# Two layers of adapters, attention and routed experts on one core: second expert products in seven quarter products, first adapter matrix in four pieces

## The chip, the cores and the metric

The kernel runs on 1 core of one Trainium2 chip. The metric is the device time in microseconds (us) of one execution. Three runs of the kernel before took 1205.24, 1205.88 and 1206.55 us; the median is 1205.88 us.

A core has a matrix engine (TensorE, PE in the profile; PEld is its loading of weights), VectorE (DVE), ScalarE (ACT), GpSimd (POOL) and SyncE (SP, which only starts transfers here). Each engine works through its own instructions in order. They wait for each other by counters: an instruction that needs another engine's result waits until that engine's counter has reached a number. TensorE writes its results into an accumulation memory (PSUM), from which VectorE or ScalarE fetch them.

## The reference

`x` is 8 sequences of 128 rows by 512, in f32, as everything here. Cut to what matters:

```python
# layer 0: one adapter matrix of eight per sequence, then a base matrix with 8 experts (2 per row)
c = einsum('bsi,boi->bso', x, weight[adapter_ids])
x = x + (c @ base_w.T + base_b + 2 * experts(c))
# layer 1: attention with 32 heads over a paged cache of 512 and the row itself, then 64 small experts
y = attention(x, ...)                                      # 8 x 128 x 512
scores = (y @ Wq_w.T) @ keys.T                             # 64 experts
gate = softmax over the 16 best, 0 elsewhere
z = (y @ A_w.T) * gate, each expert's gate over its 8 columns   # first product, 8 x 128 x 512
x = x + 2 * (z @ B_w.T)                                    # second product and residual
```

The last line is the second product of the title: eight products of 128x512 by 512x512, to which the rows that layer 0 left are added.

## The kernel before, in words

**Layer 0** (the head, the first 120 us or so). Eight sequences `b` are worked off in eight steps `t`. `l0_load(b)` starts the transfers of the transposed rows `xT` and of the adapter matrix `wt` (1 MB, its number read from `ids` into a register); for `b == 0` the matrix comes in three pieces (256, 256 and 512 KB), all by SP's queue, and `xT` by ACT's. On PE stand per step the adapter products (L626, `cp`), the transposed expert row of the step before (L683, `ltp`), its product (L689) and the base products (L643, L648). On VectorE stand the gate of the two experts (L653 to L671, ending with `low`, which L683 turns), then the sum `x1` (L691) and its scale. Between them lie pieces of side work: `l0_rows` (L567 to L571) computes the row numbers for the value cache from `vpg`, and `l0_angles(0..3)` computes the angles for the rotation from `leni` and `fr`. `l0_small` has POOL start the transfers of `leni`, `fr`, `vpg` and `nw` in this order, behind the sum of rows and bias (L677). At t = 1 the order on VectorE is gate, `l0_rows`, one product on `nw`, `l0_angles(0)`.

**Layer 1.** 64 units `u` (a sequence and a head group each) run as a pipeline written out by hand: `iteration(u)` holds scores, softmax, exchange through DRAM, values and output products of up to four units. PE is fed without a break by this order. The last iterations (`u` = 64 to 66, NU is 64) hold the rest of the pipeline and the experts of layer 1 for seven of eight sequences: `f_turn` (transposed rows, L857), `f_project` (first product, L866), `f_gate` (the gate on VectorE, L877 to L899). The gated `z` of sequences 0 to 5 is transposed by an exchange through DRAM (`z_blocks`, `z_exchange`), and `z_turn` copies it on ScalarE (L393) to the form that PE takes; that of 6 and 7 is transposed on PE (L919). `spare` is the memory of the layer's transposed input `xo`, free by then.

**The tail** (from 1171.7 us). `f_second(t)` is the second product of one sequence: 4 matmuls of 128 columns by 512 into one PSUM tile, then on VectorE `ot = op + x1` (L1452), with the rows `x1` loaded by SP shortly before (L1421), and a store by SP (L1455). The tiles come from the tags "o" and "y" in turn. The last sequence goes in two halves of 256 columns, each into a tile of its own and with its own sum and store. Between the products stand `f_turn`, `f_project` and `f_gate` of sequence 7, and the transposes of 6 and 7. An f32 matmul stands in the profile as two records: the 4 matmuls of a sequence are 8.

PSUM is given out in tiles: `bank(tag)` is 128x512 f32 for one of the tags "o", "y", "q", "kv"; `banks()` is twice that, for one of two places in turn. The framework puts the waits between engines into the program, by the tiles that instructions read and write.

## Time and profile before

| | |
|---|---|
| median of 3 runs | 1205.88 us |
| profiled execution: its time, its span | 1209.55 us, 1207.8 us |
| PE busy in the span | 1194.7 us (99%) |
| VectorE, ScalarE, POOL busy | 913.1, 504.3, 740.4 us |
| granted TensorE clock | 1.000 |
| DMA, mean | 250 GB/s |
| PE's idle time, startup included | 13.1 us |

The span is the time from the first to the last instruction of the profiled execution; its time is longer by 1.75 us, and it is one of the slower executions (the median is 3.67 us below it). A row of a timeline has start, duration, engine, line, operation, what is written from what, shape, and behind it in brackets the idle time before and what ended it. Since matmuls are pipelined, the start of one and the start of the next lie closer together than the duration of one: 16 records of 128x128 in 1.95 us, where one takes 0.28.

### The profile page before, as it was taken

The numbers are of one execution on the slowest core, as the hardware profiler recorded it, in microseconds if no ns is written. First come the engines' busy times: TensorE is split into PE (matmuls) and PEld (weight loads), VectorE is DVE, ScalarE is ACT, GpSimd is POOL, SyncE is SP. The second block draws the span as 40 slices with busy tenths as digits, with TensorE's granted clock in tenths as the row PEclk, the third lists the DMA queues.
The fourth block names the chain that finished last, engine by engine and source line by source line (L and its number), as shares of the span: only waits on it lengthen the run. The fifth ranks groups of instructions, "written<-read, shape, count | busy, mean of one in ns | idle before, by whom it ended". The sixth has DMA issues, their size and how long they took to land.

```text
span 1207.8 us, 16783 instructions
## 1 busy us (share of the span) xinstructions
PE 1194.7 (99%) x4156; PEld 714.6 (59%) x4156; DVE 913.1 (76%) x2103; ACT 504.3 (42%) x1457; POOL 740.4 (61%) x828
## 2 busy tenths in 40 slices
PE   9999999999999999999999999999999999999998
PEld 7666545565555556555556555555656555555554
DVE  2647788787888787878887887879887888787632
ACT  1345534443444444444444444444444444443211
POOL 3545769778755686578647685687657784643100
PEclk9999999999999999999999999999999999999999
DMA  8823777888888988888789978887989888898742
GB/s 315 287 89 113 247 238 245 263 265 264 264 253 257 301 244 278 260 287 282 237 258 282 294 240 281 285 289 246 279 255 302 254 263 251 261 281 230 232 140 97
DMA packets 205300, 302.31 MB, mean 250 GB/s; under 512 B 84755, under 2 KB 119316, under 8 KB 204180
## 3 DMA queue, kind: packets, MB, share of 16 engines
q1 hardware_dynamic: 170308, 196.81, 53.2%
q10 hardware_dynamic: 18576, 52.04, 13.6%
q0 software_dynamic: 16320, 52.40, 12.4%
q8 instruction: 33, 0.54, 0.2%
q14 instruction: 63, 0.52, 0.1%
HBM read 185.44 MB, written 115.74 MB: 249 GB/s over the span
## 4 chain that ended last, share of the span: by engine, by line
PE 82%; DMA 6%; POOL 4%; DVE 3%; issue 2%; SPq 1%; ACT 1%; ACTq 0%; DVEq 0%; POOLq 0%
PE o L956 18%; PE p L262 18%; PE s L439 16%; PE y L1081 13%; PE s L442 4%; PE p L295 3%; DMA px<-pb 2%; PE op L1445 2%; PE y L1094 2%; PE bp L648 1%; PE cp L626 1%; DMA kt<-in_kc 1%; PE fr L866 1%; POOL p L469 1%; DVE pb L474 1%
## 5 line engine op out<-in xcount | busy, mean ns | idle before, releaser
L463 ACT ACTIVATE p<-p,low 128x640 f32<-128x640 f32 x256 | 211.8, 828 | 433.7 <-DVE den L468 267.4
L469 POOL TENSOR_SCALAR p<-p,den 128x640 f32<-128x640 f32 x256 | 210.2, 822 | 233.4 <-DVE den L468 232.5
L452 DVE CUSTOM_DVE_ANT_0 p<-s,mask,rs 128x640 f32<-128x640 f32 x256 | 222.3, 878 | 81.6 <-PE s L442 80.7
L262 PE MATMUL p<-wqkv,xo 128*128 128x384 f32 x784 | 281.1, 487 | 0.7 <-DVE c L265 0.3
L439 PE MATMUL s<-kt,qkT 128*128 128x512 f32 x504 | 258.7, 595 | 4.5 <-DMA kt<-in_kc 2.6
L956 PE MATMUL o<-pT,vt 128*128 128x512 f32 x512 | 230.2, 592 | 0.0
L474 DVE STREAM_TRANSPOSE pb<-p 128x640 f32<-128x640 f32 x248 | 204.8, 826 | 25.6 <-POOL p L469 25.5
L1081 PE MATMUL y<-wo,oT 128*128 128x256 f32 x784 | 206.6, 380 | 0.9 <-DVE yp L1168 0.5
L262 PEld LDWEIGHTS p<-wqkv,xo 128*128 128x128 f32 x784 | 148.2, 190 | 70.2 <-POOL wqkv L163 1.6
L442 PEld LDWEIGHTS s<-qkT 128*128 128x128 f32 x504 | 95.8, 190 | 120.5 <-issue 120.5
L203 POOL DMA_INDIRECT vt<-in_vc,vrow x128 | 137.6, 1075 | 40.8 <-issue 31.9
L956 PEld LDWEIGHTS o<-pT,vt 128*128 128x128 f32 x512 | 97.2, 190 | 107.8 <-issue 92.8
L439 PEld LDWEIGHTS s<-kt,qkT 128*128 128x128 f32 x504 | 94.2, 190 | 78.3 <-issue 32.5
L1081 PEld LDWEIGHTS y<-wo,oT 128*128 128x128 f32 x784 | 131.9, 191 | 9.8 <-PE s L442 1.2
L311 ACT ACTIVATE sq<-c 128x128 f32<-128x128 f32 x320 | 98.8, 309 | 9.5 <-DVE oT L474 1.4
L442 PE MATMUL s<-qkT 128*128 128x128 f32 x504 | 96.8, 274 | 0.0
L317 POOL TENSOR_TENSOR rs<-ss,mhalf 128x5 f32<-128x5 f32 x64 | 82.2, 1284 | 5.3
L979 ACT COPY oT<-o 128x512 f32<-128x512 f32 x64 | 37.4, 585 | 102.3 <-PE o L956 77.2
L315 POOL TENSOR_SCALAR ss<-ss,eps 128x5 f32<-128x5 f32 x64 | 27.6, 431 | 74.3 <-ACT sq L311 74.3
L956 PE MATMUL o<-pT,vn 128*128 128x512 f32 x128 | 65.4, 592 | 0.0
L425 DVE STREAM_TRANSPOSE pb<-ca 128x640 f32<-128x640 f32 x60 | 50.2, 836 | 18.1 <-DMA px<-pb 8.2
L265 DVE TENSOR_TENSOR c<-c,p 128x384 f32<-128x384 f32 x84 | 44.9, 534 | 22.9 <-PE p L262 22.7
(198 smaller groups left out, 1441.3 us busy)
## 6 DMA issues: line engine op xcount, KB each, us to landing
pT<-px SPq DMA_DIRECT2D x64, 1280.0 KB, 6.6
px<-pb SPq DMA_DIRECT2D x120, 400.0 KB, 5.2
px<-pb ACTq DMA_DIRECT2D x120, 400.0 KB, 4.2
qkb<-px SPq DMA_DIRECT2D x60, 320.0 KB, 3.4
kt<-in_kc SPq DMA_DIRECT2D x512, 32.0 KB, 5.1
wqkv<-in_wqkv POOLq DMA_DIRECT2D x32, 384.0 KB, 4.8
wo<-in_wo POOLq DMA_DIRECT2D x17, 512.0 KB, 7.5
yd<-yp POOLq DMA_DIRECT2D x12, 512.0 KB, 9.0
```

What stands on the lines that cost most here:

```text
L203: nc.gpsimd.indirect_dma_start(out=kv_t[step][1][:, c, :], out_offset=None, in_=vc, in_offset=bass.IndirectOffsetOnAxis(ap=vrow[:, hf, at ...
L262: nc.tensor.matmul(out=ps, lhsT=xo[:, pr, x, c, :], rhs=w[:, c, :], start=(c == 0), stop=(c == 1))
L311: nc.scalar.activation(sq, cs[:, at : at + D], AF.Square, accum_out=ss[:, h : h + 1])
L317: nc.gpsimd.tensor_tensor(rs, ss, mhalf, ALU.pow)
L439: nc.tensor.matmul(out=s[:, :L], lhsT=qkT[:, h, :], rhs=kt[:, :, g % GH, :], start=True, stop=True)
L442: nc.tensor.matmul(out=s[:, L:NK], lhsT=qkT[:, h, :], rhs=qkT[:, REP, :], start=True, stop=True)
L452: nc.vector.tensor_tensor_reduce(out=p, in0=s_t.pop((u, h))[:, :NK], in1=mask_t[st], scale=rs_t[u][:, h : h + 1], scalar=BIG, op0=ALU.add, ...
L463: nc.scalar.activation(p, p, AF.Exp, bias=low, scale=-1.0, accum_out=den)
L469: nc.gpsimd.tensor_scalar(p_t[u, h], p_t[u, h], den, 1.0, ALU.mult, ALU.mult)
L474: nc.vector.transpose(pb_t[u][:, :, h * w : (h + 1) * w].rearrange("p i (j a) -> p j i a", a=32), p_t.pop((u, h)).rearrange("p (j i a) -> ...
L956: nc.tensor.matmul(out=o, lhsT=vt[:, c, j * D : (j + 1) * D] if c < LC else vn_t.pop(u), rhs=pT[:, c], start=(c == 0), stop=(c == LC),)
L1081: nc.tensor.matmul(out=y_t["y"][:, half * HN : (half + 1) * HN], lhsT=part(key)[:, i * S : (i + 1) * S], rhs=wo_t[:, slot(w, key[0] // (B ...
```

## The change

In the **head**, the first adapter matrix comes in four pieces of 256 KB, the first and third by SP's queue and the second and fourth by ACT's, each engine with the matrix number in a register of its own. And `l0_rows` moves from t = 1 to t = 2, behind `l0_angles`.

In the **tail**, the second products are computed for pairs of sequences. The `z` of a pair stands as four quarters (two sequences by two halves of the inner 512), the matrix as four quarters (two halves of the inner by two of the outer 512); seven products of sums of quarters, M1 to M7, give what eight quarter products gave (Strassen's scheme in Winograd's form). `f_quarters` computes four sums of the matrix on POOL at u = 64, `z_sums(p)` four sums of the pair's `z` on POOL. `f_product(p, n)` is one product: 2 matmuls by 256 columns into half a PSUM tile, then on VectorE one sum that adds the result to one to four of the pair's residual quarters, in place. The residual rows are loaded into `spare` in iterations 65 and 66. Each pair takes one `banks()` tile for its first four products, a "o" tile for the next two and a "y" tile for the last.

```diff
-            a = nc.sync.value_load(ids[0:1, b : b + 1])
-            at = (0, P, 2 * P, DM) if b == 0 else (0, DM)
-            for n, end in zip(at, at[1:]):
-                nc.sync.dma_start(
+            both = (nc.sync, nc.scalar) if b == 0 else (nc.sync,)
+            which = [e.value_load(ids[0:1, b : b + 1]) for e in both]
+            at = range(0, DM + 1, P if b == 0 else DM)
+            for i, (n, end) in enumerate(zip(at, at[1:])):
+                both[i % len(both)].dma_start(
...
-            if t == 1:
+            if 1 <= t <= 4:
+                l0_angles(t - 1)
+            if t == 2:
                 l0_rows()
                 nc.vector.tensor_scalar_mul(nw[:, 0, :], nw[:, 0, :], -SCALE)
-            if 1 <= t <= 4:
-                l0_angles(t - 1)
...
+    def f_quarters():
+        b = fw_t["b"]
+        q11, q12, q21, q22 = (b[:, 2 * i : 2 * i + 2, j * HN : (j + 1) * HN] for i in (0, 1) for j in (0, 1))
...
+        tt = nc.gpsimd.tensor_tensor
+        tt(t3, q22, q12, ALU.subtract)
+        tt(t2, t3, q11, ALU.add)
+        tt(t4, q21, t2, ALU.subtract)
+        tt(t1, q12, q11, ALU.subtract)
+        fw_t["q"] = [q11, q21, q22, t4, t1, t2, t3]
+
+    def z_sums(p):
...
+        a11, a12, a21, a22 = a[:, :2], a[:, 2:], b[:, :2], b[:, 2:]
+        tt = nc.gpsimd.tensor_tensor
+        tt(s1, a21, a22, ALU.add)
+        tt(s2, s1, a11, ALU.subtract)
+        tt(s4, a12, s2, ALU.subtract)
+        tt(s3, a11, a21, ALU.subtract)
+        zs_t[p] = [a11, a12, s4, a22, s1, s2, s3]
...
+                for b in range(4 * z, 4 * z + 4):
+                    f_load_x(b)
...
+            if u == NU:
+                f_quarters()
...
-                nc.vector.tensor_tensor(
-                    ot[:, k : k + n], op[:, k : k + n], x1[:, k : k + n], ALU.add
+        INTO = {
+            M1: slice(0, 4),
+            M2: slice(0, 1),
+            M3: slice(1, 2),
+            M4: slice(2, 3),
+            M5: slice(1, 4, 2),
+            M6: slice(1, 4),
+            M7: slice(2, 4),
+        }
+
+        def f_product(p, n):
+            halves = at_t.setdefault(p, [])
+            if not halves:
+                two = banks(f"op_{p}")
+                halves += [two[:, i * HN : (i + 1) * HN] for i in range(4)]
+                for tag in ("o", "y"):
+                    t = bank(tag, f"op_{p}{tag}")
+                    halves += [t[:, :HN], t[:, HN:]]
+                halves.pop()
+            ps = halves.pop(0)
+            for c in range(2):
+                nc.tensor.matmul(
+                    out=ps,
+                    lhsT=zs_t[p][n][:, c, :],
+                    rhs=fw_t["q"][n][:, c, :],
...
+            x1 = spare[:, (TURNED + 2 * p) * DM : (TURNED + 2 * p + 2) * DM]
+            o = x1.rearrange("p (k n) -> p k n", k=4)[:, INTO[n]]
+            nc.vector.tensor_tensor(o, o, ps.unsqueeze(1).to_broadcast([P, o.shape[1], HN]), ALU.add)
...
+        def begin(p):
+            for n in (M1, M2, M4, M5):
+                f_product(p, n)
+
+        def end(p):
+            for n in (M6, M3, M7):
+                f_product(p, n)
+            f_store(2 * p)
+            f_store(2 * p + 1)
...
+        z_sums(1)
+        begin(0)
+        yT = f_turn(b7, sb, psum)
+        end(0)
+        z_sums(2)
+        ps = f_project(b7, yT, sb, psum)
+        f_gate(b7, *ps, sb, psum)
+        begin(1)
+        end(1)
+        for b, tag in ((b7 - 1, "q"), (b7, "kv")):
+            z_turn(b, p2.tile([P, NC, S], F32, tag=f"zT{b}", name=f"fzT_{b}"), tag)
+        begin(2)
+        end(2)
+        z_sums(3)
+        for n in (M1, M2, M6, M5, M7, M3):
+            f_product(3, n)
+        f_store(6)
+        f_store(7, 1)
+        f_product(3, M4)
+        f_store(7, 0)
```

More of the change, by code (lines that the diff above doesn't have):

```diff
@@ L504, in l0_load @@
             wt = wt_home.pop(b)
-            a = nc.sync.value_load(ids[0:1, b : b + 1])
-            at = (0, P, 2 * P, DM) if b == 0 else (0, DM)
-            for n, end in zip(at, at[1:]):
-                nc.sync.dma_start(
+            both = (nc.sync, nc.scalar) if b == 0 else (nc.sync,)
[3 more added lines that the diff above has]
+                both[i % len(both)].dma_start(
                     out=wt.rearrange("p o n -> p (o n)")[:, NC * n : NC * end],
-                    in_=w0[ds(a, 1), :, NC * n : NC * end].rearrange("e p n -> p (e n)"),
+                    in_=w0[ds(which[i % len(both)], 1), :, NC * n : NC * end].rearrange("e p n -> p (e n)"),
                 )
@@ L905, in f_gate, with z_turn, f_load_x @@
         zg_t[b] = zg
-    zT_t = {}
+    zT_t, zs_t, x1_t = {}, {}, {}
     TURNED = B - 2
-    def z_turn(b, sb):
+    def z_turn(b, zT, tag=None):
         zg = zg_t.pop(b)
         if b < TURNED:
-            zT = zT_t[b] = sb("zT", [P, NC, S])
             turn_chunks(zT, zg)
-            return
-        tp = bank("q" if b % 2 else "kv", f"ztp_{b}")
-        for c in range(NC):
-            nc.tensor.transpose(tp[:, c * S : (c + 1) * S], zg[:, c * P : (c + 1) * P], ident)
-        zT = sb("zT", [P, NC, S])
-        nc.scalar.copy(zT.rearrange("p c s -> p (c s)"), tp)
-        zT_t[b] = zT
+        else:
+            tp = bank(tag, f"ztp_{b}")
+            for c in range(NC):
+                nc.tensor.transpose(tp[:, c * S : (c + 1) * S], zg[:, c * P : (c + 1) * P], ident)
+            nc.scalar.copy(zT.rearrange("p c s -> p (c s)"), tp)
+        zT_t[b] = zT
+    def f_load_x(b):
+        at = (TURNED + b) * DM
+        x1_t[b] = spare[:, at : at + DM]
+        nc.sync.dma_start(out=x1_t[b], in_=x1_d[ORDER[b]])
+    def f_quarters():
+        b = fw_t["b"]
+        q11, q12, q21, q22 = (b[:, 2 * i : 2 * i + 2, j * HN : (j + 1) * HN] for i in (0, 1) for j in (0, 1))
+        room = [wo_t[:, i].rearrange("p (t c n) -> p t c n", t=2, c=2) for i in (3, 6)]
+        t3, t2, t4, t1 = (room[i // 2][:, i % 2] for i in range(4))
+        tt = nc.gpsimd.tensor_tensor
[5 more added lines that the diff above has]
+    def z_sums(p):
+        a, b = zT_t.pop(2 * p), zT_t.pop(2 * p + 1)
+        at = p % 3 * 2 * DM
+        room = spare[:, at : at + 2 * DM].rearrange("p (k c s) -> p k c s", k=4, c=2)
+        s1, s2, s3, s4 = (room[:, i] for i in range(4))
+        a11, a12, a21, a22 = a[:, :2], a[:, 2:], b[:, :2], b[:, 2:]
[5 more added lines that the diff above has]
+        zs_t[p] = [a11, a12, s4, a22, s1, s2, s3]
+    spare = xo.rearrange("p r x c s -> p (r x c s)")
     with ExitStack() as l1:
@@ L1247, in adaln_ffn_kernel @@
         }
-        spare = xo.rearrange("p r x c s -> p (r x c s)")
         written_t = {}
@@ L1306, in iteration @@
                 z = u - NU - 1
-                z_turn(z, lambda n, shape: wo_t[:, slot(T4, NQ - 1), z * DM : (z + 1) * DM].rearrange("p (c s) -> p c s", c=NC))
+                z_turn(z, wo_t[:, slot(T4, NQ - 1), z * DM : (z + 1) * DM].rearrange("p (c s) -> p c s", c=NC))
+                for b in range(4 * z, 4 * z + 4):
+                    f_load_x(b)
             if u >= NU:
                 z_blocks(u - NU + 4)
+            if u == NU:
+                f_quarters()
             if u in (2, 3):
@@ L1402, in adaln_ffn_kernel @@
         sm = l2.enter_context(tc.tile_pool(name="f_s", bufs=3))
-        x1_t, first_t = {}, {}
-        def home(b):
-            def sb(n, shape):
-                pool = p2 if n in ("yT", "zg", "zT") else sm
-                return pool.tile(shape, F32, tag=n, name=f"f{n}_{b}")
-            t = banks(f"fp_{b}")
-            def psum(n, shape):
-                v = t[:, DM : DM + shape[1]] if n == "z" else t[:, :DM] if n == "tp" else t[:, : shape[1]]
-                return v.rearrange("p (c s) -> p c s", c=NC) if n == "tp" else v
-            return sb, psum
@@ L1419, in f_load_x @@
-        def f_load_x(b):
-            x1 = p2.tile([P, DM], F32, tag="x1", name=f"fx1_{b}", bufs=4)
-            nc.sync.dma_start(out=x1, in_=x1_d[ORDER[b]])
-            x1_t[b] = x1
-        def f_begin(b):
-            sb, psum = home(b)
-            first_t[b] = f_turn(b, sb, psum), sb, psum
-        def f_first(b):
-            yT, sb, psum = first_t.pop(b)
-            f_gate(b, *f_project(b, yT, sb, psum), sb, psum)
-        def f_turn_z(t):
-            b = t
-            sb = lambda n, shape: p2.tile(shape, F32, tag=n, name=f"f{n}_{b}")
-            z_turn(b, sb)
@@ L1437, in f_second @@
-        def f_second(t):
-            b = t
-            zT, x1 = zT_t.pop(b), x1_t.pop(b)
-            ot = p2.tile([P, DM], F32, tag="ot", name=f"ot_{t}")
-            n = DM // 2 if t == B - 1 else DM
-            for k in range(0, DM, n):
-                op = bank("kv" if k else "y" if t % 2 else "o", f"op_{t}_{k}")
-                for c in range(NC):
-                    nc.tensor.matmul(
-                        out=op[:, k : k + n],
-                        lhsT=zT[:, c, :],
-                        rhs=fw_t["b"][:, c, k : k + n],
-                        start=(c == 0),
-                        stop=(c == NC - 1),
-                    )
-                nc.vector.tensor_tensor(
-                    ot[:, k : k + n], op[:, k : k + n], x1[:, k : k + n], ALU.add
-                )
-                nc.sync.dma_start(out=out[ORDER[b], :, k : k + n], in_=ot[:, k : k + n])
-            if t + 4 < B:
-                f_load_x(t + 4)
@@ L1459, in adaln_ffn_kernel, with sb, psum @@
-        z_exchange(TURNED)
-        for t in range(4):
-            f_load_x(t)
-        f_second(0)
-        f_begin(7)
-        f_turn_z(2)
-        f_second(1)
-        f_first(7)
-        for t in range(3, B):
-            f_turn_z(t)
-            f_second(t - 1)
-        f_second(B - 1)
+        b7 = B - 1
+        def sb(n, shape):
+            pool = p2 if n in ("yT", "zg") else sm
+            return pool.tile(shape, F32, tag=n, name=f"f{n}")
+        def psum(n, shape):
+            t = bank({"tp": "kv", "r": "q", "z": "kv"}[n], f"fp_{n}")
+            return t[:, : shape[1]] if len(shape) == 2 else t.rearrange("p (c s) -> p c s", c=NC)
@@ new lines, in room4 @@
+        def room4(z):
+            t = kvp.tile([P, 2 * DM], F32, tag="kt", name=f"fzT_{z}")
+            return [t[:, i * DM : (i + 1) * DM].rearrange("p (c s) -> p c s", c=NC) for i in range(2)]
+        at_t = {}
+        M1, M2, M3, M4, M5, M6, M7 = range(7)
+        INTO = {
[7 more added lines that the diff above has]
+        }
@@ new lines, in f_product @@
+        def f_product(p, n):
[13 more added lines that the diff above has]
+                    rhs=fw_t["q"][n][:, c, :],
+                    start=(c == 0),
+                    stop=(c == 1),
+                )
+            x1 = spare[:, (TURNED + 2 * p) * DM : (TURNED + 2 * p + 2) * DM]
+            o = x1.rearrange("p (k n) -> p k n", k=4)[:, INTO[n]]
+            nc.vector.tensor_tensor(o, o, ps.unsqueeze(1).to_broadcast([P, o.shape[1], HN]), ALU.add)
@@ new lines, in f_store @@
+        def f_store(b, half=None):
+            at = slice(0, DM) if half is None else slice(half * HN, (half + 1) * HN)
+            nc.sync.dma_start(out=out[ORDER[b], :, at], in_=x1_t[b][:, at])
+        def begin(p):
[6 more added lines that the diff above has]
+            f_store(2 * p + 1)
+        z_exchange(TURNED)
+        z_sums(0)
+        for p in (1, 2):
+            for b, zT in zip((2 * p, 2 * p + 1), room4(p)):
+                z_turn(b, zT)
```

## The prediction

> **What bounds the kernel now.** I read the page first, then PE's waits, the rows of the tail, and the rows that price a hand-over between engines.

> ```profile
> PE 1194.7 (99%) x4156; PEld 714.6 (59%) x4156; DVE 913.1 (76%) x2103; ACT 504.3 (42%) x1457; POOL 740.4 (61%) x828
> PE 82%; DMA 6%; POOL 4%; DVE 3%; issue 2%; SPq 1%; ACT 1%; ACTq 0%; DVEq 0%; POOLq 0%
> ```

> PE is busy nearly always and carries the chain that ends last. So time is won where PE does less or idles less, and lost where PE is made to wait. The tail, from the timeline:

> ```profile
> 1171.75 3.60 PE L1445 MATMUL op<-fw,wo 128*128 128x512 f32 x8
> ...
> 1175.19 0.60 PE L857 MATMUL fp<-ident,ya 128*128 128x128 f32 x4
> ...
> 1179.06 4.04 PE L866 MATMUL fp<-fw,fyT 128*128 128x320 f32 x16
> ...
> 1200.99 3.21 PEld L1445 LDWEIGHTS op<-fw,fzT 128*128 128x128 f32 x15 [0.24 <-issue]
> 1204.64 0.42 DVE L1452 TENSOR_TENSOR ot<-op,fx 128x256 f32<-128x256 f32 x1 [1.30 <-PE op L1445]
> ```

> PE goes without a gap. A record of 512 columns takes 0.429 us to the next (8 from 1171.75 to 1175.19), one of 256 takes (3.21 - 0.19) / 14 = 0.2157; a turn of four transposes 0.43, the first product of sequence 7 (1179.06 to 1182.94) 3.88. The last sum ends at 1205.06, 33.31 after the first product's start, which I call T0. The sums of L1452 lie beside PE: no product waits for one, because each goes to a tile of its own.

> The head, from the waits of PE, VectorE and SP:

> ```profile
> PE cp L626 <- DMA wqkv<-in_w: 1.2, 1, 1.2
> PE ltp L683 <- DVE low L671: 0.9, 1, 0.9
> DVE vpg L568 <- DMA vpg<-in_vpages: 3.2, 1, 3.2
> SPq L503 <- DMA wqkv<-in_w: 2.2, 1, 2.2
> ```

> **The tail, step 1: work on PE.** Before: 56 records of 0.429 and 16 of 0.2157 are 27.47 us. After: 4 pairs x 7 products x 4 records x 0.2157 = 24.16. Run without gaps, that saves 3.3.

> **Step 2: the waits added.** The built program of the changed kernel shows PE's order with its waits. In pairs 0 to 2, M2 waits for VectorE's count after M1's sum, M4 for that after M2's, M5 for that after M4's, M3 for that after M6's. In pair 3: M2 for M1, M6 for M2, M5 for M6, M3 for M7. The rule in it: a product that goes into a tile waits until the sum of the product before it in that tile has read it, though the columns differ. Queued behind each waiting product is all of PE's work, and the tail ends with PE. So the sums come onto the path. Their durations, from the same kind of sum in the pipeline (residual plus PSUM result spread over quarters):

> ```profile
> L1150 DVE TENSOR_TENSOR yp<-yp,y 128x512 f32<-128x512 f32 x28 | 18.2, 649 | 0.0
> L1150 DVE TENSOR_TENSOR yp<-yp,y 128x256 f32<-128x256 f32 x42 | 17.3, 412 | 0.0
> L1150 DVE TENSOR_TENSOR yp<-yp,y 128x768 f32<-128x768 f32 x14 | 12.8, 916 | 0.0
> L1150 DVE TENSOR_TENSOR yp<-yp,y 128x1024 f32<-128x1024 f32 x10 | 11.8, 1182 | 0.0
> ```

> A hand-over back to PE, where a product waited for a VectorE sum, beside a group of the same kind that did not:

> ```profile
> 154.72 0.52 DVE L265 TENSOR_TENSOR c<-u,p 128x384 f32<-128x384 f32 x1
> 155.28 1.56 PE L262 MATMUL p<-wqkv,xo 128*128 128x384 f32 x4 [0.33 <-DVE c L265]
> 165.84 1.45 PE L262 MATMUL p<-wqkv,xo 128*128 128x384 f32 x4
> ```

> The sum ends at 155.24, PE starts 0.04 later, and the group is 0.11 longer, for the weights that could not be loaded ahead. The other way: the last record of the tail starts at 1204.22, takes 0.38, and L1452 starts 0.04 after its end. So a product that waits has its own sum start 0.04 + 0.11 + 3 x 0.2157 + 0.38 + 0.04 = 1.22 after the sum it waited for.

> One pair, from its first matmul: M1's sum (1024 wide) from 1.07 to 2.25; M2's (256) 3.46 to 3.88; M4's (256) 5.09 to 5.50; M5 starts at 5.65, M6 right behind at 6.52, its sum (768) from 7.58 to 8.50; M3 starts at 8.65, M7 at 9.51, PE is free at 10.38. Two sequences took 6.86 before; without waits a pair would take 6.04. In pair 3 the order is another: sums of M1 to 2.25, M2 to 3.88, M6 (768) to 6.01; M5 starts at 6.16, M7 at 7.02, its sum (512) ends at 8.74; M3 starts at 8.89, M4 at 9.75, M4's sum ends at 11.23.

> **Step 3: the gate in VectorE's queue.** Pair 0, the turn and the project of sequence 7 end at T0 + 10.38 + 0.43 + 3.88 = 14.69. The gate starts when the first half of the project is there (10.81 + 7 x 0.27 + 0.43, about 13.2; it now has its own tile) and takes 3.57 (1183.21 to 1186.78 before), to 16.73. M1's sum of pair 1 would start at 15.76 and stands behind it: 1.0 more. Pair 1 ends at 26.07, two turns at 26.93, pair 2 at 37.31, the last sum at 48.54. Against 33.31: **15.2 longer**. Each of the 16 hand-overs may be 0.1 off either way: 13.6 to 16.8.

> **Step 4: what is covered.** POOL: `f_quarters` is 4 sums of 512 (1.27 each), begun when POOL falls idle at 1137.9, needed at T0 + 4. It may hold up two small VectorE sums of a gate (L664 took 0.88 instead of 0.17 beside a POOL sum), 2.5 at most, with 10 us until the next project. `z_sums` is 4 sums of 256 (0.73 each) per pair; pair 0's begin at 1168.7, when L393 has copied sequence 1, and s1 is needed at T0 + 5.65; pair 3's 2.9 lie under pair 2. Were that cover gone, a pair would cost up to 2.9 more. SP's eight loads of residual rows (0.43 each) stand ahead of the last exchange read, by 1.7; what it feeds on ScalarE precedes the copy of sequence 7's turn, needed at T0 + 10.8, over 10 us later. The last store now follows 384 KB issued within 0.9 us (before: 128 KB 1.7 us earlier): 0 to 1.0, the fastest slice of the tail being 387 GB/s; I take 0.2, since 128 KB landed in 1.7.

> **Step 5: the head.** VectorE waited 3.2 for `vpg` ahead of L691, whose product (L689) was done at 31.1 while L691 started at 33.16; so L683 started at 38.19 where PE was free at 37.12 (16 records of 0.1117 from 35.33). With `l0_rows` a step later the angles come first; `leni` and `fr`, issued at 20.1 and 20.6, landed 5.2 and 6.1 later, before VectorE gets there at 27.1. The moved operations (1.2 us) then stand between `low` and the next L691, where about 3 us are free. Gain 1.07, at least 0. The matrix: 32 records of 0.1117 from 6.03 would end at 9.60; they end at 9.54 + 16 x 0.1117 = 11.33, so at most 1.72 is to be had, and not less than 0: the same 1024 KB are issued no later. Next late is the second adapter matrix: SP saw it land at 15.9 and PE takes it at 17.02, which leaves 1.1, my value. ScalarE's two issues and register load now precede its table load (1.28), with the first copy at 11.63. Together -2.2, between -2.8 and 0, carried on by a PE that is full.

> Sum: 15.2 + 0.2 - 1.1 - 1.1 = +13.2. The profiled span would become 1221.0 and its time 1222.8; that execution lies 3.67 above the median, which becomes **1219.1**.

> [...] For the clock the trace has:

> ```profile
> 6.00:9.50 3.50, 2.24 (x18) 1.86 (x16) 0.00 (x0) 0.00 (x0) 0.00 (x0) 1.00 0.97 337
> 160.00:164.00 4.00, 2.40 (x8) 1.01 (x7) 2.65 (x7) 0.58 (x1) 2.79 (x3) 1.00 0.93 309
> ```

> PE was busy 64% and 60% of these stretches, and the granted clock (third number from the right) stayed 1.00; in the tail I expect 58% and idle times up to 2.4.

> **Rivals.** (a) *Faster*: PE runs the tail dense: -3.3 + 0.2 - 2.2, 1200.6. Its place is `f_product`. A wait for a sum is harmless from the point where PE has other work between two products of a tile, as long as hand-overs and sum: 0.16 + 0.04 + sum + 0.15, so 0.8 to 1.5 us. For it speaks that the columns differ; against it that the program has the waits and that nothing stands between M1 and M2 or M2 and M4. 0.04. (b) M4 (M6 in pair 3), which lies in the other half of the double tile, goes without its wait: 0.78 less per pair by the rows above, 1216.0; against it again the program. 0.04. (c) The granted clock falls to half in the tail: its records (24.2 + 3.9 us) take twice their time, up to 1247, and 1233 if half the tail is struck; the two stretches above speak against it. 0.06. (d) The matrix in four pieces brings nothing, the transfers being bound by what the 16 engines move: 1220.2, within my range. The forecast, (d) with it, has 0.86. Only (a) ends on the other side.

> **How the numbers follow.** Low end: hand-overs -1.6, head -0.6 and half the spread of the three runs, -0.65, make 1216.3; with (b) 1216.0. High end: hand-overs +1.6, head +2.2, store +0.8, runs +0.65 would make 1224.3; since all four seldom come together, 1223.8. A measurement of this kernel can tell about 0.2% (2.4 us) from no change. Faster has (a), 0.04, the same 0.01, slower the rest, 0.95.

> **What would show it.** In the tail: 16 waits of PE for the new sum's line, each 0.6 to 2.2 us of idle time; PE busy near 60%; sums of 0.41 to 1.18; some 48.5 us from the first product to the last sum; the clock at 1.00. In the head: no wait for `vpg`, L683 without its 0.9, the second half of the first product before 9.5. Wrong would be: PE dense in the tail; products of one tile that start before the sum ahead of them ends; or a lower clock there.

## The result, and the profile after

The changed kernel takes **1227.69 us** (median of 6 runs, 1223.38 to 1233.33), the kernel before in the same session 1206.83 (6 runs): a ratio of 1.0174, 95% interval 1.0154 to 1.0194. The direction and the added waits were forecast; the time lies 8.6 us above the forecast and 3.9 above the top of its range.

The profiled execution of after is the slowest of its six, 1233.33 us with a span of 1231.6, so its own time is 5.6 above the median. From its page: PE's busy time and the chain that ended last.

```profile
PE 1201.9 (98%) x4196; PEld 724.4 (59%) x4196; DVE 928.6 (75%) x2122; ACT 503.5 (41%) x1457; POOL 759.4 (62%) x848
PE 87%; DMA 3%; DVE 3%; POOL 3%; issue 2%; ACT 1%; SPq 1%; ACTq 0%; DVEq 0%; POOLq 0%
```

PE's busy time went **up** by 7.2, though its work in the tail went down by 3.3. So records of PE must have got longer somewhere; the windows below show where. PE's waits, in us altogether, number and longest:

```profile
PE op L1474 <- DVE xo L1483: 11.3, 12, 2.3
PE s L439 <- DMA kt<-in_kc: 3.6, 3, 1.9
PE cp L627 <- DMA wqkv<-in_w: 1.5, 1, 1.5
...
PE op_2o L1474 <- DVE xo L1483: 1.1, 1, 1.1
PE op_0o L1474 <- DVE xo L1483: 1.1, 1, 1.1
PE op_1o L1474 <- DVE xo L1483: 1.1, 1, 1.1
...
PE op_3o L1474 <- DVE xo L1483: 0.8, 1, 0.8
```

Those of L1474 for the new sum's line number 12 + 4 = 16, the forecast number. The wait for `vpg` is gone, and with it L683's 0.9. The matrix wait was not shortened in this profile: it moved from the middle of the first product to its front. The first product of pair 0 starts at 1173.75, the last sum ends at 1228.68: the tail takes **54.93 us**, where 48.54 were forecast and 33.31 stood before.

Of the 6.4 us that the forecast misses, 5.6 are in pair 1 and the two turns behind it. First VectorE, then PE, from the timeline (start, busy, engine, line, tiles, idle time before and its releaser):

```profile
1190.44 0.41 DVE L900 TENSOR_TENSOR fzg<-fp_z,fwf 128x256 f32<-128x256 f32 x1
1190.77 1.21 DVE L1483 TENSOR_TENSOR xo<-xo,op 128x1024 f32<-128x1024 f32 x1
```

```profile
1188.75 1.03 PE L1474 MATMUL op<-fw,fzT 128*128 128x256 f32 x4
1192.04 1.50 PE L1474 MATMUL op<-fw,fzT 128*128 128x256 f32 x4 [2.26 <-DVE xo L1483]
1194.06 2.07 PE L1474 MATMUL op<-wo,fzT 128*128 128x256 f32 x4 [0.51 <-DVE xo L1483]
```

As forecast, M1's sum stands behind the gate (whose last row is L900) and PE idles 2.26. But then the same four records take 1.50 and 2.07 instead of 1.03. The windows view shows a granted clock of 0.50 there. Its columns are: stretch, length, busy us of PE, PEld, VectorE, ScalarE and POOL, the granted clock, DMA share, GB/s. The trace of after records changes of the clock at 161.84, 165.25, 1192.66 and 1206.31 us, which lie 1, 301 and 4 times 3.413 apart; the stretches, called windows here, are cut at this step.

```profile
1189.25:1192.66 3.41, 1.15 (x6) 0.70 (x5) 2.60 (x7) 0.00 (x0) 0.00 (x0) 1.00 0.00 0
1192.66:1196.08 3.42, 2.91 (x7) 1.34 (x5) 0.42 (x1) 0.00 (x0) 0.00 (x0) 0.50 0.00 0
1196.08:1199.49 3.41, 2.81 (x8) 2.22 (x8) 1.10 (x2) 0.00 (x0) 0.00 (x0) 0.50 0.00 0
1199.49:1202.90 3.41, 2.27 (x6) 1.40 (x5) 0.97 (x2) 0.00 (x0) 0.00 (x0) 0.50 0.00 0
1202.90:1206.31 3.41, 3.41 (x12) 2.74 (x12) 1.11 (x2) 0.05 (x1) 0.00 (x0) 0.50 0.20 77
1206.31:1209.73 3.42, 2.11 (x12) 1.54 (x10) 1.22 (x1) 1.08 (x2) 2.11 (x3) 1.00 0.20 77
```

In the first window PE is busy for 1.15 of 3.41 us, a share of 0.34. The next four windows run at half clock, and so pair 1 takes 16.4 us (1188.75 to 1205.17) instead of the forecast 11.4, and the turns 1.4 instead of 0.9. The same happened once in the pipeline, 158.42 to 165.25: a wait of 1.9 for `kt`, a window in which PE was busy for 0.43 of it (1.48 of 3.41), then one at a clock of 0.50.

So the theory after the result: (i) the tile waits serialise PE and VectorE, as forecast; (ii) the four windows at 0.50 come from the one window of low PE share (0.34) ahead of them, made by the gate in VectorE's queue; (iii) the head brings less than forecast. The rivals: the clock falls for another reason (the head's edits, chance); or PE and VectorE hold each other up in PSUM whatever the tile.

### The profile page after: what moved, and what is told of

Read it like the earlier page. It is cut to its first block, busy times and chain, and to the rows that moved or that the text cites. A ratio compares the mean times of both kernels' runs of the same rounds, so it can differ in the third digit from the quotient of the medians.

```text
span 1231.6 us, 16932 instructions
## 1 busy us (share of the span) xinstructions
PE 1201.9 (98%) x4196; PEld 724.4 (59%) x4196; DVE 928.6 (75%) x2122; ACT 503.5 (41%) x1457; POOL 759.4 (62%) x848
## 4 chain that ended last, share of the span: by engine, by line
PE 87%; DMA 3%; DVE 3%; POOL 3%; issue 2%; ACT 1%; SPq 1%; ACTq 0%; DVEq 0%; POOLq 0%
PE o L986 19%; PE p L262 18%; PE s L439 16%; PE y L1111 12%; PE s L442 4%; PE p L295 3%; PE cp L627 2%; PE y L1124 2%; PE bp L649 2%; DMA kt<-in_kc 2%; PE op L1474 1%; PE fr L867 1%; DVE xo L1483 1%; PE fz L867 1%; POOL wqkv L163 1%
## 5 line engine op out<-in xcount | busy, mean ns | idle before, releaser
L262 PE MATMUL p<-wqkv,xo 128*128 128x384 f32 x784 | 281.2, 487 | 0.5 <-POOL wqkv L163 0.4
L262 PEld LDWEIGHTS p<-wqkv,xo 128*128 128x128 f32 x784 | 148.1, 190 | 70.4 <-POOL wqkv L163 2.2
L425 DVE STREAM_TRANSPOSE pb<-ca 128x640 f32<-128x640 f32 x60 | 50.1, 836 | 18.2 <-DMA kt<-in_kc 11.9
L265 DVE TENSOR_TENSOR c<-c,p 128x384 f32<-128x384 f32 x84 | 44.9, 534 | 23.3 <-PE p L262 23.1
```

The source lines that it names most:

```text
L262: nc.tensor.matmul(out=ps, lhsT=xo[:, pr, x, c, :], rhs=w[:, c, :], start=(c == 0), stop=(c == 1))
```

## Experiments

Each ran beside the kernel before (medians 1206.82, 1206.68 and 1206.93 in the three sessions). A "half window" is a stretch of 3.413 us at a granted clock of 0.50, which is what half clock means here. "Tail" is from the first matmul of the products to the end of the last sum.

**Head alone, tail alone.** `head_only` is the kernel before with the first two parts of the diff; `tail_only` is the changed kernel without them.

```diff
# head_only, against before
-            if t == 1:
+            if 1 <= t <= 4:
+                l0_angles(t - 1)
+            if t == 2:
                 l0_rows()
...
-            at = (0, P, 2 * P, DM) if b == 0 else (0, DM)
+            at = range(0, DM + 1, P if b == 0 else DM)
```

> The kernel before with only the two edits of the head (four matrix pieces by two queues, l0_rows a step later); the tail is the old one. Theory 'the head's gain is carried to the end': 1.07 for the rows and 0.4 for the pieces, 1.5 less, 1205.3 us. Rival 'the middle eats it' (PE waits for kt at units 3 and 4, one clock window of 3.41 us at half speed near 162 us, then a drift of some 2 us, as the profile of the changed kernel has them): 1206.8 + 2.0 = 1208.8, with a granted clock below 1.00 near 162 us. If the middle's loss belongs to the tail's edits instead (their loads and POOL work start late), nothing of it is here and the clock is 1.00 up to the last window.

Measured: 1205.86 (11 runs), ratio 1.000, interval 0.998 to 1.0019: 1.0 less by the medians, and not to be told from none. That lies nearer to the theory's 1205.3 than to the rival's 1208.8. In its profile the clock was 1.00 up to the end, in the middle too, so the head's edits do not by themselves bring a half window.

> The kernel before with only the new tail (quarter products, residuals in place); the head is the old one. Theory 'waits by tile plus a halved clock': first product to last sum between 48.5 us (clock 1.00) and 55 us (four half-clock windows in pair 1), against 33.3 before: 1206.8 + 15.2 + 0.2 = 1222.2 without the clock's share, 1228.6 with that of the profiled run, and a spread of several us from run to run, since the windows' place against the gate's idle time is free. Rival 'the clock is struck by the head's edits': 1222.2 in every run, spread within 0.3%, clock 1.00 in the tail.

Measured: 1226.19 (5 runs, 1223.50 to 1227.71), ratio 1.0158 (1.0131 to 1.0184). The tail took 52.27 and its clock fell with the old head too, again behind the gate:

```profile
1183.14:1186.56 3.42, 1.13 (x4) 0.68 (x4) 2.16 (x5) 0.00 (x0) 0.00 (x0) 1.00 0.00 0
1186.56:1189.97 3.41, 2.60 (x5) 1.68 (x6) 0.57 (x2) 0.00 (x0) 0.00 (x0) 0.50 0.00 0
1189.97:1193.38 3.41, 3.22 (x8) 2.03 (x6) 0.84 (x2) 0.00 (x0) 0.00 (x0) 0.50 0.00 0
```

PE is busy for 0.33 of the first window, and two windows at half clock follow; behind the second of them, in which PE was busy for 0.94, the clock is full again. The loss belongs to the tail's edits.

**More work in the idle time.** Sixteen transposes that nobody reads, once in the wait behind the gate, once where PE does not wait.

```diff
# fill_gate, in f_product ahead of M2 of pair 1
+            w = 16 if (p, n) == (1, M2) else 0
+            if w:
+                t = banks(f"fill_{p}_{n}", turn_of[0])
+                for i in range(w):
+                    nc.tensor.transpose(t[:, :S], ident, ident)
# fill_late: the same 16 transposes ahead of begin(2) instead
```

> The changed kernel with 16 transposes of the identity into an unused PSUM tile (1.79 us of PE work whose output nobody reads) between M1 and M2 of pair 1, in the 2.26 us in which PE waited for M1's sum behind the gate. Theory 'a window of 3.41 us with PE busy 0.34 halves the clock': that window rises to about 0.85, the clock stays 1.00 through pair 1, which takes 11.4 instead of 16.4; 1227.7 - 5.0 = 1222.7 us, and the spread between runs shrinks: more work, less time. Rival 'the clock falls for another reason': 1227.7 as before, 1229.5 if the added records stand in the way.

Measured: **1221.70** (6 runs), 6.0 less than the changed kernel with 1.79 us more work. Tail 49.53. PE's rows, and its window:

```profile
1180.90 1.03 PE L1479 MATMUL op<-fw,fzT 128*128 128x256 f32 x4
1181.77 1.91 PE L1477 MATMUL fill<-ident 128*128 128x128 f32 x16
1184.19 1.13 PE L1479 MATMUL op<-fw,fzT 128*128 128x256 f32 x4 [0.51 <-DVE xo L1488]
```

```profile
1181.51:1184.92 3.41, 2.90 (x21) 2.51 (x21) 2.52 (x6) 0.00 (x0) 0.00 (x0) 1.00 0.00 0
```

PE is busy 0.85 of the window and the clock stays 1.00. Two of the six runs (1225.87 and 1230.88) still had a mean clock of 0.993 and 0.992, which is five to six half windows; where, their times do not say. That left open whether they had lost them in other waits of the tail.

> The changed kernel with the same 16 transposes (1.79 us of work nobody reads), but put where PE waits for nothing: ahead of the first product of pair 2. Theory 'the low window behind the gate halves the clock, and only work inside that window keeps it': PE's idle 2.26 us in pair 1 stay, the clock still falls there, and the transposes come on top: 1227.7 + 1.8 = 1229.5 us (1228 to 1231). Rival 'any added PE work in the tail keeps the clock up, or the 1221.7 of the other place had another cause': 1221.7 to 1223.5.

Measured: 1231.77 (6 runs, 1227.86 to 1239.45). That is far from the rival by which any added work helps, and 0.8 above the top of what was expected. In its profile PE is busy for 0.46 of the gate's window, and three half windows follow, of which this is the first:

```profile
1184.52:1187.93 3.41, 1.57 (x6) 1.09 (x7) 1.69 (x3) 0.00 (x0) 0.00 (x0) 1.00 0.00 0
1187.93:1191.34 3.41, 2.81 (x8) 1.76 (x7) 0.42 (x1) 0.00 (x0) 0.00 (x0) 0.50 0.00 0
```

All six runs had a mean clock of 0.985 to 0.996. So the time fell where the transposes lie in the low window (1221.70) and rose where they are added elsewhere (1231.77).

**All waits filled.**

```diff
# fill_all, in f_product ahead of each product that waits
+            w = ({M2: 8, M6: 3, M5: 7, M3: 5} if p == 3 else
+                 {M2: 16 if p == 1 else 8, M4: 3, M5: 3, M3: 8}).get(n, 0)
```

> The changed kernel with transposes of the identity (0.11 us each, output read by nobody) in all 16 places where PE waits for a sum: 16 behind the gate, 8, 3, 5 or 7 elsewhere, each a little less than the idle time measured there. Theory 'PE's busy share alone decides the clock, the waits the rest': with no window below 0.6 the clock is 1.00 in the tail of every run, and the two of six runs that still lost five windows with the filler at the gate alone do not come up; 49.5 us from first product to last sum as there, 1221.0 to 1222.0 us and all runs within 5 us. Rival 'those two runs lost theirs elsewhere': a median of 1221.7 as with the gate's filler, with runs near 1226 to 1231 again.

Measured: 1222.67 (5 runs, 1218.81 to 1223.67), clock 1.000 in every run, tail 49.54. The median is 0.7 above the expected range, but the spread is the expected one and no run came up at 0.992; five runs are few to say that none would. So the changed kernel takes about 1222.7 at full clock, and the clock's part of its time is 1227.7 - 1222.7 = **5.0 us** by the medians, from few runs, whose ranges overlap by 0.3 (1223.38 is the lowest of the changed kernel, 1223.67 the highest here). The profiles agree: against the 49.54 of this tail, the tail is longer by 5.4 with four half windows (after), by 2.7 with two (`tail_only`) and by 55.66 - 49.54 - 1.79 = 4.3 with three (`fill_late`), so about 1.4 for each.

**A tile for each product.** Everything else is as in the changed kernel; the products, and between them the turns and the project of sequence 7, take six places of PSUM in turn.

```diff
# own_tiles
+        place_of = [0]
+        def place(name):
+            i = place_of[0] % 6
+            place_of[0] += 1
+            if i < 2:
+                return banks(name, i)[:, :DM]
+            return bank(("o", "y", "q", "kv")[i - 2], name)
...
-            ps = halves.pop(0)
+            ps = place(f"op_{p}_{n}")[:, :HN]
```

> The changed kernel, with one thing else: each of the 28 products, the turn and the project of sequence 7 takes the next of six PSUM tiles in turn (the two double ones, o, y, q, kv), so that a product waits for the sum six places back and not for the one just before it. Theory 'the wait comes from sharing a tile': PE runs the tail dense, four pairs of 6.04, turn and project 4.31, turns 0.86, the last hand-over 0.45: 29.8 us from first product to last sum against 33.3 before; clock 1.00; 1206.8 - 3.5 + 0.2, and -1.5 to +2.0 for head and middle: 1202.0 to 1205.5 us, 1203.8 likeliest. Rival 'VectorE is the bound' (its sums, 4.65 a pair, and the gate): pairs of 6.1 to 7, 1206 to 1208. Rival 'PE and VectorE hold each other up in PSUM whatever the tile': 48.5 us stay, 1219 or more.

Measured: **1202.62** (11 runs), ratio 0.9963 (0.9947 to 0.9979): faster than the kernel before, and 25 us faster than the changed one. PE's timeline in pair 1:

```profile
1179.59 1.89 PE L1474 MATMUL op<-fw,fzT 128*128 128x256 f32 x8
1181.32 1.03 PE L1474 MATMUL op<-wo,fzT 128*128 128x256 f32 x4
1182.18 1.89 PE L1474 MATMUL op<-wo,xo 128*128 128x256 f32 x8
```

No row has an idle time in brackets: M1 and M2 are one group of 8 records, and the next starts 1.73 after it, 8 x 0.2157. The tail takes 29.99, against 33.31 before and 54.93 with shared tiles. The sums last as long as in the changed kernel (1.22, 0.95, 0.69, 0.42) and hold up nobody. Both rivals fall: VectorE is not the bound, and with six tiles PE shows no idle time beside VectorE's reads of PSUM.

Its profile shows the fall of the clock far from the tail, too: PE idled 2.28 us in the pipeline, was busy 0.33 of a window, and the next ran at 0.50.

```profile
677.17:680.58 3.41, 1.13 (x5) 0.61 (x5) 1.91 (x6) 0.67 (x2) 2.83 (x4) 1.00 1.00 281
680.58:683.99 3.41, 3.41 (x10) 2.20 (x9) 1.03 (x4) 0.92 (x2) 1.98 (x2) 0.50 0.93 253
```

The same with the old head (`own_tiles_oldhead`):

> The new tail with six PSUM tiles in turn, and the old head. Theory 'head and tail add up, the head's lead is carried to the end': 1.5 more than the 1202.6 with both, 1204.1 us, PE 1.5 later at its first attention unit. Rival 'the head's lead is swallowed by waits in the middle': 1202.6 as with both.

Measured: 1203.45 (12 runs), ratio 0.9975 (0.9959 to 0.9991); tail again 29.99. The head is worth 0.8 by the medians of the two, between the two expectations and too little to decide for either; and PE was 0.2 later at its first attention unit, not 1.5 (below).

**How many tiles.** Products by turns into two, or three, single tiles, all else as in the changed kernel.

```diff
# two_tiles; three_tiles has ("o", "y", "q") and % 3
-            ps = halves.pop(0)
+            place_of[0] += 1
+            ps = bank(("o", "y")[place_of[0] % 2], f"op_{p}_{n}")[:, :HN]
```

> The changed kernel with the products going by turns into two PSUM tiles (o and y), so that a product waits for the sum two places back. Theory 'a wait costs hand-over plus sum less the work that PE has in between': with the measured sums (1.22, 0.95, 0.69, 0.42) and 0.86 a product, PE still idles 0.73 before M4, 0.2 before M6, 0.26 to 0.46 before M3, 1.3 in pair 1 behind the gate: 35.5 us from first product to last sum against 30.0 with six tiles and 54.9 (49.5 at full clock) with the shared ones; no window of PE below 0.5, so clock 1.00: 1202.6 + 5.5 = 1208.1 us. Rival 'any wait at all costs the full hand-over, or strikes the clock': 1213 or more. Rival 'two are as good as six': 1203.

Measured: 1208.62 (12 runs), ratio 1.0017 (1.0002 to 1.0031), tail 36.33 where 35.5 was worked out, clock 1.00. The wait price by distance (hand-over plus sum, less the work between) holds to a microsecond.

> The changed kernel with the products going by turns into three PSUM tiles (o, y, q), so that two other products (1.73 us) lie between a product and the sum it waits for. Theory 'hand-over plus sum (0.8 to 1.6 us) less the work between': nothing is left but 0.4 behind the gate: 30.4 us from first product to last sum, 1203.0 us, as with six tiles. Rival 'something else than the count of places made six dense': 1205 or more.

Measured: 1206.10 (12 runs), tail 33.09 where 30.4 was expected. It is a miss, and the time is the rival's (1205 or more); PE's waits name what it was.

```profile
PE op L1467 <- DVE fzg L900: 1.8, 1, 1.8
PE ztp L919 <- DVE xo L1476: 0.8, 1, 0.8
PE op L1467 <- DVE ya L1180: 0.8, 1, 0.8
```

My working had counted the products alone. But the third tile, `q`, also takes the first half of sequence 7's project, which the gate reads last (L900), and a turn; and `y` takes the last output product, read by L1180. The first two lie in the tail: 30.4 + 1.8 + 0.8 = 33.0. With the third, 1203.0 + 3.4 = 1206.4.

**The parts of the head.** `pieces_only` and `rows_only` are the kernel before with one of the two edits, with one run each.

> The kernel before with only the matrix in four pieces by two queues. By the head of the changed kernel's profile: the first product is 0.4 earlier, and the wait for vpg at about 35 us is as before, so PE's first attention unit is 0.4 earlier (forecast was 1.1); the rest of 1.5 then belongs to the moved rows. One time of 1203 to 1209 us says nothing on this.

Measured: 1204.90; no wait in the middle of the first product, one of 0.5 ahead of it, and L684 (the old L683) idle for 0.4. The first exponential of unit 0, ScalarE's first step for the first attention unit, lies at 88.17, within what the head varies.

> The kernel before with only l0_rows a step later. In the profiles so far the first attention unit's first exponential lies at 87.6 to 87.9 us with both edits of the head and at 87.9, 89.3 and 89.5 with neither, 88.2 with the pieces alone. Theory 'the vpg stall (0.9 of PE in one profile, none in two others) is what the rows edit takes away, the matrix wait stays': no stall near 37 us, a wait of 0.8 to 2.1 us after the first half of the first product, 87.9 to 89.3. Rival 'the rows edit alone makes the head the same each time': 87.7.

Measured: 1207.39; no stall near 37 us, and the matrix waits 0.7 and 1.9. But the first exponential lies at 91.08, outside both expectations. The windows:

```profile
7.78:11.19 3.41, 1.50 (x12) 1.31 (x13) 0.00 (x0) 0.00 (x0) 0.00 (x0) 1.00 0.98 386
11.19:14.61 3.42, 3.42 (x17) 3.20 (x17) 0.00 (x0) 0.54 (x1) 0.00 (x0) 0.50 1.01 417
```

The matrix wait left PE busy 0.44 of a window, and the next one ran at half clock with PE busy throughout, by my estimate 1.7 us more (half of its 3.42).

Over all profiles the first exponential of unit 0 lies at 89.46, 89.27 and 87.87 with the old head (before, `tail_only`, `own_tiles_oldhead`), a mean of 88.87, and between 87.57 and 87.93 in eight with both edits, a mean of 87.71. So the head's edits bring 1.2 on average, and with them the head takes nearly the same time in each profile. What the two waits of the old head cost does not add up: where the matrix came 2.05 late (`tail_only`), the `vpg` stall was gone, since PE came to L683 after `vpg` anyway.

## Why the prediction was right and wrong

- **Step 1 (3.3 us less work on PE): right.** With the waits gone, the tail is 33.31 - 29.99 = 3.3 shorter. The change's idea is sound; only where it puts its products undoes it.
- **Step 2 (waits by tile): right, a little small.** All 16 waits, in the forecast places. Rival (b)'s 3.1 is shown by no run: in after, M4 (M6 in pair 3) has its wait in all four pairs, with 0.51 to 0.61 of idle time. The tail at full clock is 49.5 (`fill_gate`, `fill_all`), 1.0 above the forecast 48.54; the sums were 0.01 to 0.04 longer than the rows they were priced from, and the rest must be in the hand-overs, which were not measured one by one.
- **Step 3 (M1's sum of pair 1 behind the gate): right in time, wrong in its consequence.** PE idled 2.26 there, as the terms give. That this one idle time falls in one 3.41 us window and takes its busy share to 0.34 was the step that I did not make.
- **Rival (c), the halved clock: this is the step that failed.** It had 0.06 and belonged into the forecast. Two errors in it. I set the mean of the whole tail (58%) against stretches at 60 and 64%, but in the runs it was single windows that were followed by a lower clock: in the changed kernel, windows of the tail at 0.54 to 0.75 kept the clock at 1.00 (1206.31 to 1226.79; in `fill_gate` two at 0.67), and the one at 0.34 was followed by 0.50. And between the startup and the end, the trace of before has no window below 0.59 (159.11 to 162.52, PE busy 2.03 of 3.41), so its two stretches could not exclude a fall at 0.34. The half stands in that trace at one place only: its last window with matmuls (1203.56 to 1206.97, PE busy 1.04 of 3.41) is followed by a granted clock of 0.50, where nothing was left to run. What the runs showed in place of the 1.00 that was forecast is a clock of 0.50 behind the gate's window, at a price of 5.0 us at the median. With its waits filled and the clock at 1.000 the changed kernel takes 1222.7 (`fill_all`), which is inside the forecast range.
- **Step 4 (covers): right.** POOL's sums and the loads hid: no wait of PE in the tail for them, and nothing but the 16 waits. From the last sum's end to the span's end it is 2.9 after, 2.7 before: the 0.2 taken.
- **Step 5 (the head, -2.2): the second term mis-sized.** `head_only` brought 1.0 and the two kernels with six tiles differ by 0.8; by the head's own rows it is 1.2. In the profile of after the matrix wait goes from the middle of the first product to its front (1.5), and the product ends 0.4 earlier where I took 1.1. The delay of L683 by `vpg` is not in every run (1.07, 0.1 and 0 with the old head), so the 1.07 was one execution's number. Nor was "carried on by a PE that is full" to be relied on: PE waits 0.6 to 1.9 for `kt` near 160 us in every profile, in after's long enough for a half window. The tail's first product starts anywhere between 1165.9 and 1173.7 us in the thirteen profiles, which is far more than the head's 1.2.

The sum with measured terms, without the clock: 1219.1 + 1.2 (head 1.0 for 2.2) + 1.0 (hand-overs) = 1221.3, where `fill_all` measured 1222.7. Of the 1.4 between them, 0.95 is the starting point: the forecast went out from a median of 1205.88 for the kernel before, and its six runs in the session of the result have 1206.83. The clock's 5.0 make up the rest to 1227.7 by the way they were taken. The six runs span 10 us. In the gate's window PE idles 2.26 in after and 1.84 in `fill_late`; that the windows' place against the gate differs so from run to run too may be why, but no experiment shows it, and the mean clock alone does not order them (runs at 0.994 took 1225.0 to 1232.1).

Rival (a), the dense tail, is what the kernel could have had: the condition given for it, other work between two products of a tile as long as hand-over and sum, is what six tiles fulfil.

## What to carry to other kernels

When products that PE could run back to back are read by another engine, give each a PSUM tile of its own, as many in turn as hand-over plus read takes PE to fill (here 0.8 to 1.6 us against 0.86 per product), and count every other user of those tiles, gates and turns too. When a change adds waits to PE, find in the trace at what step it records changes of the clock (3.413 us here), cut the stage at that step and look at the lowest window, not at the mean: here windows with PE busy for 0.33 to 0.46 were followed by one to four at 0.50, and in the tail each of these cost about 1.4 us. A gain in the head of one execution should be checked against how that head varies from run to run.

## What the runs showed of the hardware

```profile
8.98:12.39 3.41, 1.92 (x16) 1.86 (x16) 0.00 (x0) 0.00 (x0) 0.00 (x0) 1.00 1.02 422
```

- At a clock of 0.50, windows with PE busy for 0.67 to 0.85 of them were followed by another at 0.50 (0.85, 0.82 and 0.67 in after, 0.76 in `tail_only`, 0.82 and 0.67 in `fill_late`), and those with 0.94 (`tail_only`) or 1.0 (after twice, `fill_late`) by 1.00. At a clock of 1.00, windows with 0.62 to 0.67 (after, 1206.31 to 1219.96) were followed by 1.00. One low window was followed by four half windows in the tail of the changed kernel, and by one in the pipeline, where PE is busy throughout the next.
- Work that is thrown away shortened this kernel: 1.79 us of transposes in the low window took 6.0 us off the median, and the same transposes elsewhere added 4.1, of which 1.8 are their own length and the rest is within the spread of the runs.
